# A four-image conv, state-space scan and expert layer on one core: the work beside the scans is cut finer and placed anew

## The chip, the cores and the metric

The kernel runs on one core of a Trainium2 chip. Five engines work side by side and meet at semaphores: PE (TensorE, matmuls and transposes into PSUM), DVE (VectorE), ACT (ScalarE), POOL (GpSimd) and SP, which here only issues DMAs. The metric is the device time of one execution in microseconds (us), as the median of several runs; a difference between two kernels is judged by such medians.

## The reference, cut to what matters

Input is `x` of 4 images of 32x32 pixels with 256 channels, all float32. Layer 0, the part that the change touches:

```python
x = layernorm(src) @ w_in + b_in              # 256 -> 512 channels
x = gelu(depthwise_conv_3x3(x, conv_w) + conv_b)
x = x.reshape(B, 1024, 512)
dt_raw, Bm, Cm = split(x @ w_x, [16, 80])     # 16 + 64 + 64 columns
dt = softplus(dt_raw @ w_dt + dt_bias)
def step(h, (xt, dtt, Bt, Ct)):               # over 1024 pixels, 64 states a channel
    h = exp(dtt * A) * h + (dtt * xt) * Bt
    return h, sum_n(h * Ct)
y = scan(step) + x * D_skip
out = src + layernorm(y) @ w_out + b_out
```

Layer 1 is an attention in matrix form and a mixture of 16 experts, two to a token. It follows layer 0, and the change leaves it alone.

## The kernel before

**Units and steps.** Each image is cut into two halves of 512 pixels, so there are 8 *units*, in order image by image. Units 0, 2, 4, 6 are first halves ("even"), units 1, 3, 5, 7 second halves ("odd"). Within a unit the 64 states are taken one after another: a *step* is one state n of one unit, 512 steps in all. Channels lie on the partitions in 4 groups of 128 (m = 0 to 3). A step therefore has 4 *slots*, one for each m, and a unit has 256 slots, numbered `at` in the code; `k` counts slots over all units.

**What one step does.** ACT makes `da = exp(dt*A)` for each m (`decay`, L901), 128x512. The input of the scan, `dt*x*B[n]`, is made row-major, in four row blocks j of 128 pixels, and then transposed by PE into a PSUM bank `ps` (`turn`, L908 and L913). A row block is scaled by ACT (`scale`, L881, tile `bx`, ten buffers). The first row block (j = 0) has three kinds: "A" it is scaled by ACT like the others; "P" it is scaled by POOL (`scale_apart`, L892, tile `bxp`); "D" it isn't scaled at all, but PE multiplies `dtxT` by a diagonal matrix of B that was written to DRAM and fetched again (`fetch_diagonal`, L873, tile `dgb`). DVE runs the scan itself, 128x512 (L927), from `da` and `ps` into `h`, a ring of four steps. After the fourth scan of a step POOL multiplies `h` by C (L934, 128x2048, with `cb_n`, which SP fetches as a broadcast of 256 KB a step). Eleven slots after a scan PE transposes `h` and sums it in four PSUM banks `y` (`add_up`, L948). There are three banks for `ps` and one, `bg`, for all work beside the scans, so that only one piece of that work can hold PSUM at a time.

**The work beside the scans.** While unit u is scanned, the inputs of later units are made: the layernorm and first product of a half image (`head`: ACT, PE, a copy, then PE and a copy into `pad`), the convolution as nine PE products a channel group with diagonal taps `dgc` (`conv`, L405) and its evacuation with bias (L417 or L419), gelu, then the projections for unit u+1 (`dt_bc`: product L456, copies `put_pair` L464, `put_low` L477, `put_bc` L488, then `dt_raw` L518, `put_dt` L528 and L529, exp, log, four sums of each m on POOL L560 to L566, and the turn to `dtxT` with copy L576). For unit u-1 it makes the layernorm's statistics (`after_stats`, L275) and the output product (`after`, L644 to L669). The last unit makes the attention's matrices instead.

**How it is put in order.** Nothing is left to a scheduler: the loop over k issues, slot by slot, `scale(k+8)`, `decay(k+4)`, `scan(k)`, `turn(k+3)`, `add_up(k-11)`, the fetches, and then as many *pieces* of the work beside as fit. Each piece has the smallest number of slots after its predecessor, an engine, a cost and a callable. `beside` lays each list of pieces evenly over a range of slots (`SKIP`, `HEAD1`, `CONV0`, `CONV1`, `HEAD0`, `STATS`, `DT`, `AFTER`); a piece goes out when its slot has come, its gap is over, what it needs is done, the `bg` bank is free if it takes it, and the costs already used on its engine in this slot leave room under `MOST`. Which engine makes a copy is read from `ODD` and `EVEN` through `on_scalar`:

```python
ODD, EVEN = ("pad", "xg", "yT", "dtx"), ("xg", "yT", "dtx")
CONV0, CONV1 = (50, 236), (22, 176)
DT = ((11, 38), (51, 64), (81, 93), (94, 184), (185, 240))
SUMS = (25, 51)
LAG = 11
FIRST, MOST = 11, 1.0
```

Kinds of the first row block follow a rule: in units up to 6, steps 25 to 50 are D and A in turn; elsewhere each fourth step is D and the rest P; D is A in unit 0. So units 1 to 6 have 13 A, 28 P and 23 D steps, unit 0 has 36 A and 28 P, unit 7 has 48 P and 16 D.

Of the kernel before, what the change touches and what calls it, by code (L numbers as in the profile page):

```python
# [16 lines left out]
P = 128  # L17
# [16 lines left out]
def conv_ssm_attn_moe_kernel(ctx: ExitStack, tc: tile.TileContext, a: dict, out: bass.AP):  # L34
# [106 lines left out]
    with ExitStack() as l0:  # L141
# [101 lines left out]
        EVERY = 2  # L243
        diag_b = [dram.tile([NS // EVERY, P, P], F32, name=f"diag_b{k}") for k in range(2)]
# [3 lines left out]
        def zero_diagonals(k):  # L248
            nc.sync.dma_start(
                out=diag_b[k].rearrange("n a b -> a n b"), in_=over_middle(zero, NS // EVERY)  # L250
            )
# [65 lines left out]
        def head(b, g, lo=0, hi=TPB):  # L317

            todo = [piece(1, "SP", 0, lambda: load_head(b, g))]

            def diagonal(i):
                t = pre.tile([P, P], F32, name="dg", tag="dg", bufs=2)
                i += g * TPB
                nc.scalar.activation(t, ident, AF.Copy, scale=rs_h[:, b, i : i + 1])
                i -= g * TPB
                made["dg", i] = t

            def turned(i, ck):
                if ck == 0:
                    take()  # L330
                nc.tensor.matmul(
                    made["bg"][:, blk(ck, P)], made["xt"][:, i, blk(ck, P)], made["dg", i],
                    start=True, stop=True,
                )

            def put(i):
                if i == lo:
                    made["xT"] = pre.tile([P, CK, BANK], F32, name="xT")
                nc.vector.tensor_copy(
                    made["xT"][:, :, blk(i, P)],  # L340
                    made["bg"][:, : CK * P].rearrange("p (k t) -> p k t", k=CK),
                )

            for i in range(lo, hi):
                todo.append(piece(6 if i == lo else 1, "ACT", 0.3, lambda i=i: diagonal(i)))
                for ck in range(CK):
                    todo.append(piece(
                        0 if ck else 2, "PE", 0.22, lambda i=i, ck=ck: turned(i, ck),
                        "" if ck else "take",
                    ))  # L350
                todo.append(piece(
                    2, "ACT" if on_scalar("xT") else "DVE", 0.42, lambda i=i: put(i), "free"
                ))

            def mult(m, ck):
                if ck == 0:
                    take()
                nc.tensor.matmul(
                    made["bg"][:, : (hi - lo) * P], w_in[:, ck, blk(m, P)],
                    made["xT"][:, ck, lo * P : hi * P], start=(ck == 0), stop=(ck == CK - 1),  # L360
                )

            def put_pad(m):
                pad = pads[m][:, 1 + g * ROWS + lo * RPT : 1 + g * ROWS + hi * RPT, 1 : 1 + WW]
                bg = made["bg"][:, : (hi - lo) * P].rearrange("p (h w) -> p h w", w=WW)
                if on_scalar("pad"):
                    nc.scalar.activation(pad, bg, AF.Identity, bias=b_in[:, m : m + 1])
                else:
                    nc.vector.tensor_scalar(pad, bg, b_in[:, m : m + 1], None, ALU.add)

            for m in range(DK):
                for ck in range(CK):
                    todo.append(piece(
                        1, "PE", 0.86, lambda m=m, ck=ck: mult(m, ck), "" if ck else "take"
                    ))
                todo.append(piece(
                    3, "ACT" if on_scalar("pad") else "DVE", 0.7, lambda m=m: put_pad(m), "free"
                ))
            return todo

        def conv(v):
# [19 lines left out]
            def tap(m, k):  # L401
                if k == 0:
                    take()
                i, j = divmod(k, 3)
                nc.tensor.matmul(  # L405
                    made["bg"].rearrange("p (h w) -> p h w", w=WW),
                    made["dgc", m * 3 + i][:, j, :],
                    pads[m][:, half * ROWS + i : (half + 1) * ROWS + i, j : j + WW],
                    start=(k == 0), stop=(k == 8),
                )  # L410
# [19 lines left out]
            for m in range(DK):  # L430
                for k in range(9):
                    if k % 3 == 0 and m * 3 + k // 3 + 2 < 3 * DK:
                        todo.append(piece(
                            0, "SP", 0, lambda q=m * 3 + k // 3 + 2: taps(q)
                        ))
                    todo.append(piece(
                        2, "PE", 0.86, lambda m=m, k=k: tap(m, k), "" if k else "take"
                    ))
                todo.append(piece(
                    3, "ACT" if on_scalar("xg") else "DVE", 0.69, lambda m=m: put(m), "free"  # L440
                ))
# [3 lines left out]
        def dt_bc(w, needs):  # L445
# [15 lines left out]
            def put_pair(j):  # L461
                if j == 0:
                    made["proj", w] = acts.tile([P, TPB, RX], F32, name="proj")
                nc.vector.tensor_copy(  # L464
                    made["proj", w][:, j : j + 2, :],
                    made["bg"][:, : 2 * RX].rearrange("p (j n) -> p j n", n=RX),
                )
# [8 lines left out]
            def put_low():  # L476
                nc.vector.tensor_copy(dtr[:R, :], made["bg"][:R, :])  # L477
# [8 lines left out]
            def put_bc():  # L486
                t = pre.tile([P, BANK], F32, name="bct")
                nc.vector.tensor_copy(t, made["bg"])  # L488
                cd = dram0.tile([NS, BANK], F32, name="cd")
                nc.sync.dma_start(out=cd, in_=t[NS:, :])  # L490
                if w > 0:
                    with nc.allow_non_contiguous_dma(reason="diagonals"):
                        nc.sync.dma_start(
                            out=diag_b[w % 2].rearrange("n a b -> n (a b)")[:, :: P + 1],
                            in_=t[:NS:EVERY, :P],
                        )
                made["cd", w] = cd

            for j in range(TPB):
# [5 lines left out]
                if j % 2:  # L505
                    todo.append(piece(3, "DVE", 0.5, lambda j=j: put_pair(j - 1), "free"))
            todo.append(piece(2, "PE", 0.44, turn_low, "take"))
            todo.append(piece(3, "DVE", 0.69, put_low, "free"))
            todo.append(piece(1, "PE", 0.44, turn_bc, "take"))
            todo.append(piece(3, "DVE", 0.69, put_bc, "free"))  # L510
# [5 lines left out]
            def dt_raw(m):  # L516
                take()
                nc.tensor.matmul(  # L518
                    made["bg"], w_dt[:, blk(m, P)], dtr, start=True, stop=True
                )  # L520
# [60 lines left out]
            for m in range(DK):  # L581
                todo.append(piece(1, "PE", 0.86, lambda m=m: dt_raw(m), "take"))
# [44 lines left out]
        def after(u, need):  # L627
# [44 lines left out]
            for j in range(TPB):  # L672
# [9 lines left out]
                for m in range(0, DK, 2):  # L682
                    todo.append(piece(
                        1, "PE", 0.88, lambda j=j, m=m: (mult(j, m), mult(j, m + 1)),
# [129 lines left out]
        def on_scalar(what):  # L814

            return not alone and what in (ODD if made["u"] % 2 else EVEN)
# [39 lines left out]
        def by_diagonal(s, j):  # L856

            u, n = steps[s]
            return j == 0 and u > 0 and n % (2 if summing(u, n) else 4) == 0

        def by_pool(s, j):

            u, n = steps[s]
            return j == 0 and n % 4 > 0 and not summing(u, n)

        def summing(u, n):

            return u + 1 < len(units) and SUMS[0] <= n < SUMS[1]

        def fetch_diagonal(s):  # L870
            u, n = steps[s]
            t = scanp.tile([P, P], F32, name="dgb", bufs=3)
            nc.sync.dma_start(out=t, in_=diag_b[u % 2][n // EVERY])  # L873
# [94 lines left out]
        def beside(u):  # L968
# [4 lines left out]
            made["u"] = u  # L973
            lists = [[([
                piece(1, "PE", 0.22, lambda m=m, j=j: skip(u, m, j))
                for m in range(DK) for j in range(TPB)
            ], SKIP)]]
            if v < n:
                b, half = units[v]
                if u == 0:  # L980
                    lists.append([
                        (head(b, 0), (11, 44)), (head(b, 1), (44, 77)), (conv(v), (77, 236)),
                    ])
                elif half == 0:
                    lists.append([(head(b, 1), HEAD1), (conv(v), CONV0)])
                else:
                    lists.append([(conv(v), CONV1)])
                    if b + 1 < NB:
                        lists[-1].append((head(b + 1, 0), HEAD0))
            if v == n:  # L990
                lists.append([(matrices(), MATS)])
            if u > 0:
                lists.append([(after_stats(u - 1), STATS)])
            if u + 1 < n:
                lists.append(list(zip(dt_bc(u + 1, ("st", u - 1) if u > 0 else None), DT)))
            else:
# [4 lines left out]
                ], DT[2])])  # L1001
            if u > 0:
                lists.append(list(zip(after(u - 1, ("rs", u - 1)), AFTER)))
# [7 lines left out]
        ODD, EVEN = ("pad", "xg", "yT", "dtx"), ("xg", "yT", "dtx")  # L1011

        SKIP = (11, 24)
        HEAD1, CONV0 = (14, 85), (50, 236)
        CONV1, HEAD0 = (22, 176), (200, 240)
        STATS = (11, 69)
        DT = ((11, 38), (51, 64), (81, 93), (94, 184), (185, 240))
        AFTER = ((36, 132), (139, 229))
        MATS = (44, 245)

        SUMS = (25, 51)
        SLOTS = NS * DK
        LAG = 11
        FIRST, MOST = 11, 1.0
        with tc.manual_schedule():
# [14 lines left out]
            for k in range(n_all + LAG):  # L1040
# [5 lines left out]
                if k < n_all:  # L1046
                    scan(*divmod(k, DK))
                    if k % DK == DK - 1 and k // DK + 4 < len(steps):
                        scale_apart(k // DK + 4)
                if k + 3 < n_all:  # L1050
                    turn(*divmod(k + 3, DK))
                if k >= LAG:
                    add_up(*divmod(k - LAG, DK))
# [16 lines left out]
                while True:  # L1070
                    best = None
                    for i, l in enumerate(lists):
# [7 lines left out]
                        if used[eng] > 0 and used[eng] + c > MOST:  # L1080
# [836 lines left out]
```

## Time and profile before

| | us |
|---|---|
| median of 3 runs | 3470.42 (3470.37 to 3471.43) |
| the profiled execution, its own time | 3483.06 |
| its span, first to last instruction | 3481.3 |
| before the first scan | 131.6 |
| scans, units 0 to 7 | 131.6 to 2718.3, that is 2586.7 |
| after the scans: layer 1 and output | 763.0 |

The profile lists for each engine what it executed and for how long. Busy time of an engine in a stretch of time is the union of its instructions; the mean of one is its own length, and two neighbours on ACT, DVE or PE can overlap a little, so that their starts lie closer than that length. Times in the trace count from the first instruction. The starts of the units' first scans are at 131.6, 459.0, 784.9, 1110.4, 1435.7, 1760.0, 2084.8 and 2408.0 us.

### The profile page before, as it was taken

Reading aid. Unit: us, or ns where it says so; the run is one execution under the profiler, and the core shown is the slowest. Engines: PE = TensorE matmul, PEld = TensorE weight load, DVE = VectorE, ACT = ScalarE, POOL = GpSimd, SP = SyncE. Lnnn points to the kernel's source line nnn. Section 1 sums busy time; section 2 is a strip of 40 time slices with the busy share of each in tenths; the row PEclk is TensorE's granted clock in tenths of the full one; section 3 lists DMA queues with packets and bytes.
Section 4 is the critical chain, followed back from the end, with each engine's and each line's share of the span. In section 5 each row is a group of like instructions: output and inputs, shape, how many; then the busy total and the mean of one; then the engine's idle time right before and its main releaser. Section 6 shows DMA issues by size and latency. Waiting matters only on the chain. (4 is left out here: it accounts for less than half of the span.)

```text
span 3481.3 us, 62766 instructions
## 1 busy us (share of the span) xinstructions
PE 3205.9 (92%) x23081; PEld 2718.2 (78%) x23081; DVE 2875.8 (83%) x3290; ACT 2680.8 (77%) x4525; POOL 2690.4 (77%) x1185
## 2 busy tenths in 40 slices
PE   7989999999999999999999999889999889699995
PEld 4677877888888888878888887778777666598994
DVE  4799999999999999999999999999999676422224
ACT  1799999998999899989999998999999454221211
POOL 0489988998999899989998999999999532133331
PEclk9999999999999999999999999999999999799997
DMA  3422222222332222223222223222212100699996
GB/s 102 110 61 67 65 64 70 70 72 63 77 74 63 69 76 72 63 64 79 74 68 68 69 65 75 60 62 66 61 62 69 56 19 19 235 325 307 322 308 227
DMA packets 413577, 347.81 MB, mean 100 GB/s; under 512 B 193345, under 2 KB 299841, under 8 KB 413266
## 3 DMA queue, kind: packets, MB, share of 16 engines
q1 hardware_dynamic: 393794, 319.97, 31.9%
q0 software_dynamic: 7104, 19.41, 1.7%
q10 hardware_dynamic: 12368, 4.37, 0.5%
q8 instruction: 185, 3.03, 0.4%
q14 instruction: 126, 1.03, 0.1%
HBM read 313.65 MB, written 29.47 MB: 99 GB/s over the span
## 5 line engine op out<-in xcount | busy, mean ns | idle before, releaser
L934 POOL TENSOR_TENSOR h<-h,cb_n 128x2048 f32<-128x2048 f32 x512 | 2145.2, 4198 | 139.3 <-DVE h L927 69.2
L901 ACT ACTIVATE da<-dt,l_conv_a_log_sb 128x512 f32<-128x512 f32 x2048 | 1434.6, 712 | 76.6 <-DVE h L927 74.4
L948 PE MATMUL y<-ident,h 128*128 128x128 f32 x8192 | 1236.3, 274 | 2.5 <-POOL h L934 2.5
L927 DVE TENSOR_TENSOR_SCAN h<-da,last,ps 128x512 f32<-128x512 f32 x1024 | 1218.5, 1266 | 19.5 <-PE ps L913 11.1
L927 DVE TENSOR_TENSOR_SCAN h<-da,ps 128x512 f32<-128x512 f32 x1024 | 1163.5, 1199 | 55.0 <-PE ps L913 26.5
L881 ACT ACTIVATE bx<-dtxT,proj 128x512 f32<-128x512 f32 x1650 | 1172.5, 711 | 22.4 <-DVE dtxT L576 16.4
L913 PE MATMUL ps<-ident,bx 128*128 128x128 f32 x6600 | 1073.1, 275 | 34.4 <-DVE h L927 18.8
L948 PEld LDWEIGHTS y<-ident,h 128*128 128x128 f32 x8192 | 967.4, 142 | 3.2 <-POOL h L934 3.2
L913 PEld LDWEIGHTS ps<-ident,bx 128*128 128x128 f32 x6600 | 791.1, 142 | 141.5 <-DVE h L927 58.5
L913 PE MATMUL ps<-ident,bxp 128*128 128x128 f32 x976 | 290.7, 298 | 78.6 <-DVE h L927 64.6
L1823 DVE TENSOR_TENSOR hT<-s,p 128x256 f32<-128x256 f32 x148 | 62.4, 422 | 340.9 <-ACT s L1822 340.9
L913 PEld LDWEIGHTS ps<-ident,bxp 128*128 128x128 f32 x976 | 137.0, 140 | 223.5 <-DVE h L927 107.4
L1817 PE MATMUL p<-xT,w 128*128 128x128 f32 x2368 | 292.2, 277 | 0.5 <-ACT xT L1806 0.5
L1817 PEld LDWEIGHTS p<-xT,w 128*128 128x128 f32 x2368 | 285.7, 194 | 4.9 <-ACT xT L1806 0.9
L1837 POOL DMA_INDIRECT yd<-yb,dst x74 | 73.0, 987 | 269.2 <-DMA yd<-yb,dst 172.3
L908 PE MATMUL ps<-dgb,dtxT 128*128 128x128 f32 x1232 | 261.2, 294 | 17.9 <-DVE h L927 12.0
L908 PEld LDWEIGHTS ps<-dgb,dtxT 128*128 128x128 f32 x1232 | 195.6, 191 | 94.7 <-DVE h L927 53.3
L1822 ACT ACTIVATE s<-p 128x256 f32<-128x256 f32 x148 | 56.9, 384 | 276.1 <-PE p L1817 276.1
L405 PE MATMUL bg<-pad,dgc 128*128 128x512 f32 x432 | 221.8, 595 | 3.5 <-DMA dgc<-diags 3.0
L892 POOL TENSOR_SCALAR bxp<-dtxT,proj 128x512 f32<-128x512 f32 x244 | 170.8, 700 | 59.2 <-DVE dtxT L576 59.2
L1829 PE MATMUL pf<-w,hT 128*128 128x256 f32 x592 | 153.3, 382 | 0.1
L1786 POOL DMA_INDIRECT xb<-xd,src x74 | 71.9, 972 | 97.8 <-DMA w<-in_L_ffn_w_dram 73.8
(308 smaller groups left out, 2351.0 us busy)
## 6 DMA issues: line engine op xcount, KB each, us to landing
cb_n<-cd SPq DMA_DIRECT2D x512, 256.0 KB, 3.2
w<-in_L_ffn_w_dram SPq DMA_DIRECT2D x222, 512.0 KB, 6.0
dgc<-diags SPq DMA_DIRECT2D x84, 192.0 KB, 3.2
dgb<-diag_b SPq DMA_DIRECT2D x154, 64.0 KB, 3.1
y<-yd SPq DMA_DIRECT2D x8, 1024.0 KB, 10.3
last<-h SPq DMA_DIRECT2D x256, 2.0 KB, 2.8
diag_b<-zero SPq DMA_DIRECT2D x2, 2048.0 KB, 9.3
xd<-xe SPq DMA_DIRECT2D x8, 512.0 KB, 2.9
```

Source lines behind the costliest of these rows:

```text
L405: nc.tensor.matmul(made["bg"].rearrange("p (h w) -> p h w", w=WW), made["dgc", m * 3 + i][:, j, :], pads[m][:, half * ROWS + i : (half + 1 ...
L881: nc.scalar.activation(t, made["dtxT", u][:, j, :], AF.Copy, scale=made["proj", u][:, j, R + n : R + n + 1])
L892: nc.gpsimd.tensor_scalar(t, made["dtxT", u][:, 0, :], made["proj", u][:, 0, R + n : R + n + 1], 1.0, ALU.mult, ALU.mult,)
L901: nc.scalar.activation(t, made["dt", u][:, m, :], AF.Exp, scale=A[:, m, n : n + 1])
L908: nc.tensor.matmul(t[:, blk(j, P)], made["dtxT", steps[s][0]][:, j, blk(m, P)], made["dgb", s], start=True, stop=True,)
L913: nc.tensor.transpose(t[:, blk(j, P)], made["bx", s, j][:, blk(m, P)], ident)
L927: nc.vector.tensor_tensor_scan(h[:, m, 1:], made.pop(("da", s, m)), made.pop(("dbx", s, m)), 0.0 if seg == 0 else last[b][:, n, m : m + 1] ...
L934: nc.gpsimd.tensor_tensor(h[:, :, :BANK], h[:, :, 1:], over_middle(made["c", s], DK), ALU.mult)
L948: nc.tensor.matmul(made["y", u][j][:, blk(m, P)], made["h", s][:, m, blk(j, P)], ident, is_transpose=True, start=n == 0 and m == 0, stop=n ...
L1817: nc.tensor.matmul(p12[:, j, s, :], on[w, i][:, ck, blk(h + j, P)], on["xT", i][:, ck, :], start=(ck == 0), stop=(ck == CK - 1),)
L1829: nc.tensor.matmul(on["pf", i], on["hT", i][:, hk, :], on["w3", i][:, hk, :], start=(hk == 0), stop=(hk == HK - 1),)
L1837: nc.gpsimd.indirect_dma_start(yd[:, :], bass.IndirectOffsetOnAxis(dst[:, i : i + 1], 0), yb, None)
```

## The change

It has seven parts.

1. **Finer PE pieces.** A tap of the convolution, a product of a whole head and a product of `dt_raw` are each cut in two pieces of 256 columns; a pair of products of `after` becomes two pieces of one. The two projections of a piece of `dt_bc` stay together. The part before the scans (`alone`) keeps whole pieces.
2. **Head rows.** ACT scales the 128x256 row block itself (`scaled_rows`) instead of making a 128x128 diagonal, and PE transposes the result instead of multiplying by the diagonal.
3. **Copies.** `APART` says for even and odd units which copies ACT makes. `bc`, `low` and `pair` move from DVE to ACT in both; `xg` moves from ACT to DVE in both; `dtx` moves from ACT to DVE in even units.
4. **Kinds.** `KINDS` lists the kind of each step's first row block, for even units, odd units and the last.
5. **Diagonals.** All 64 of a unit are kept in DRAM instead of each second one, so the two clearing transfers and each unit's diagonal write are twice as large.
6. **Slots.** `EVEN`, `ODD` and `START` (unit 0) give each list its own range of slots.
7. **Order and room.** `add_up(k-11)` is issued ahead of `turn(k+3)`. `MOST` differs by engine.

By these lists the counts of A, P and D steps are: unit 0 35, 29, 0; units 2, 4, 6 23, 29, 12; units 1, 3, 5 26, 21, 17; unit 7 30, 21, 13.

```diff
-        EVERY = 2
-        diag_b = [dram.tile([NS // EVERY, P, P], F32, name=f"diag_b{k}") for k in range(2)]
+        diag_b = [dram.tile([NS, P, P], F32, name=f"diag_b{k}") for k in range(2)]
...
-            def diagonal(i):
-                t = pre.tile([P, P], F32, name="dg", tag="dg", bufs=2)
...
-                nc.scalar.activation(t, ident, AF.Copy, scale=rs_h[:, b, i : i + 1])
...
+            def scaled_rows(i):
+                t = pre.tile([P, C], F32, name="xn", tag="dg", bufs=2)
+                r = g * TPB + i
+                nc.scalar.activation(
+                    t, made["xt"][:, i, :], AF.Copy, scale=rs_h[:, b, r : r + 1]
+                )
+                made["xn", i] = t
...
+                nc.tensor.transpose(made["bg"][:, blk(ck, P)], made["xn", i][:, blk(ck, P)], ident)
...
+            cut = [(lo, hi)] if alone else [(lo, (lo + hi) // 2), ((lo + hi) // 2, hi)]
...
-                    made["bg"].rearrange("p (h w) -> p h w", w=WW),
+                    made["bg"].rearrange("p (h w) -> p h w", w=WW)[:, blk(c, deep), :],
                     made["dgc", m * 3 + i][:, j, :],
-                    pads[m][:, half * ROWS + i : (half + 1) * ROWS + i, j : j + WW],
-                    start=(k == 0), stop=(k == 8),
+                    pads[m][:, at : at + deep, j : j + WW],
+                    start=(k == 0 and c == 0), stop=(k == 8), skip_group_check=True,
...
-                    todo.append(piece(
-                        2, "PE", 0.86, lambda m=m, k=k: tap(m, k), "" if k else "take"
-                    ))
+                    for c in range(parts):
+                        todo.append(piece(
+                            1, "PE", 1.03 / parts, lambda m=m, k=k, c=c: tap(m, k, c),
+                            "" if k or c else "take",
+                        ))
...
-                            in_=t[:NS:EVERY, :P],
+                            in_=t[:NS, :P],
...
-            return j == 0 and u > 0 and n % (2 if summing(u, n) else 4) == 0
+            return j == 0 and u > 0 and KINDS[kind_of(u)][n] == "D"
...
+        APART = (
+            ('bc', 'low', 'pair', 'yT'),
+            ('bc', 'dtx', 'low', 'pad', 'pair', 'yT'),
+        )
+        KINDS = (
+            'DPPPDPPPAPPPAPPPAAPAAPPPPAPAPAPAADADDAAADAAAADADDAAADPPPDPPPDPPP',
+            'DPPPAAPAAAPAPPPAPPPAAAPAADADDADAADADADADADADADADDADPAPPPDPPPDPAP',
+            'ADADAAPAAAPAAAPAAAPADAPADAAAAPPPDAPADAPADAPAADADDPPPDPPPDPPPDAPA',
+        )
+        EVEN = {
+            'skip': (18, 66),
+            'head': (23, 91),
+            'conv': (47, 210),
+            'stats': (11, 61),
+            'dt0': (15, 21),
+            'dt1': (50, 60),
+            'dt2': (93, 97),
+            'dt3': (31, 103),
+            'dt4': (102, 214),
+            'after0': (45, 89),
+            'after1': (144, 207),
+        }
+        ODD = {
+            'skip': (13, 18),
+            'head': (179, 234),
+            'conv': (14, 172),
+            'stats': (23, 50),
+            'dt0': (17, 22),
+            'dt1': (61, 77),
+            'dt2': (90, 108),
+            'dt3': (45, 157),
+            'dt4': (221, 226),
+            'after0': (11, 104),
+            'after1': (114, 222),
+        }
...
+            'conv': (43, 228),
...
+            'dt3': (122, 188),
...
-        FIRST, MOST = 11, 1.0
+        FIRST = 11
+        MOST = {'PE': 2.1, 'DVE': 0.8, 'ACT': 1.1, 'POOL': 1.0, 'SP': 9.0}
...
+                if k >= LAG:
+                    add_up(*divmod(k - LAG, DK))
                 if k + 3 < n_all:
                     turn(*divmod(k + 3, DK))
-                if k >= LAG:
-                    add_up(*divmod(k - LAG, DK))
```

## The prediction

> **What bounds the kernel now.** I read the page's busy shares first: PE 92, DVE 83, ACT 77, POOL 77 per cent. No engine is full, yet four are nearly so, and the second part shows why: nines on all four from slice 3 to 31, which are the scans. The change touches only these, apart from eight head rows ahead of them. So I asked for busy time by unit and then by quarters of a unit (64 slots each).
>
> By unit (busy us of PE, weight loads, DVE, ACT, POOL), units 6 and 7:
>
> ```profile
> core 0: us, PE busy (x) PEld busy (x) DVE busy (x) ACT busy (x) POOL busy (x), PEclk, DMA share, GB/s
> ...
> 2084.80:2408.00 323.20, 293.65 (x2307) 259.93 (x2308) 319.43 (x297) 300.88 (x486) 304.21 (x117) 0.97 0.28 65
> 2408.00:2718.30 310.30, 290.28 (x2219) 243.43 (x2217) 308.22 (x272) 280.81 (x450) 308.58 (x123) 1.00 0.21 62
> ```
>
> DVE idles 3.8 and 2.1 us there: both are bound by DVE. In the same answer DVE's idle is 21.4, 18.3 and 18.2 us in units 0, 2, 4, and 7 us in units 1, 3, 5. The sum is 2586.7 - 2501.1 = 85.6 us. That idle is all that a better order can win. Quarters of unit 1, then of unit 2:
>
> ```profile
> 459.00:542.60 83.60, 78.76 (x625) 69.45 (x623) 82.04 (x80) 75.35 (x122) 75.77 (x30) 1.00 0.27 70
> 542.60:627.50 84.90, 81.35 (x582) 66.47 (x581) 82.30 (x74) 79.35 (x126) 77.44 (x32) 1.00 0.24 71
> 627.50:707.00 79.50, 76.78 (x588) 66.23 (x587) 76.93 (x67) 79.41 (x126) 79.50 (x30) 1.00 0.23 67
> 707.00:784.90 77.90, 75.71 (x601) 67.56 (x600) 77.58 (x71) 77.11 (x129) 77.08 (x30) 1.00 0.23 72
> ```
>
> ```profile
> 784.90:870.30 85.40, 78.17 (x624) 70.03 (x623) 82.56 (x88) 75.02 (x121) 75.16 (x29) 0.98 0.30 65
> 870.30:953.90 83.60, 81.80 (x591) 67.93 (x590) 78.56 (x75) 78.57 (x126) 78.20 (x32) 1.00 0.30 73
> 953.90:1031.30 77.40, 77.33 (x599) 68.31 (x598) 72.91 (x67) 76.48 (x125) 75.98 (x28) 1.00 0.30 74
> 1031.30:1110.40 79.10, 75.26 (x585) 67.32 (x584) 73.17 (x67) 75.68 (x120) 78.80 (x30) 0.98 0.29 70
> ```
>
> The reader is to see that the bound moves. In the first quarter DVE is full and ACT and POOL have 8 to 10 us to spare. In the second half of unit 2 DVE idles 4.5 and 5.9 us while PE, ACT or POOL is full. Whom DVE waits for, over the scans:
>
> ```profile
> DVE h L927 <- PE ps L913: 37.7, 130, 1.2
> DVE h L927 <- ACT da L901: 20.4, 28, 3.7
> DVE h L927 <- ACT bx L881: 10.2, 18, 2.9
> ```
>
> PE's part is many short waits (130, none over 1.2 us), ACT's few long ones. In the timeline such a PE wait looks like this:
>
> ```profile
> 1006.66 1.02 PE L405 MATMUL bg<-pad,dgc 128*128 128x512 f32 x2
> ...
> 1007.52 0.60 PE L913 MATMUL ps<-ident,bx 128*128 128x128 f32 x4
> ...
> 1008.33 5.69 DVE L927 TENSOR_TENSOR_SCAN h<-da,ps 128x512 f32<-128x512 f32 x5 [0.49 <-PE ps L913]
> ```
>
> A tap of the convolution holds PE for 0.86 us, the transposes for the next scan come behind it, and DVE stands for 0.49. I went through all waits of the timeline: 32 of the 37.7 us follow a tap begun within 3.5 us. Taps at their mean spacing would cover about half of the time, so the link is more than chance.
>
> [...] two 256-column products (L658) from 933.99 to the next start at 934.86 are 0.43 each, half of a 512-column tap (940.31 to 941.17, 0.86). [...]
>
> **The change part by part.**
>
> *Kinds.* An A step instead of D or P costs one more scaling on ACT. Its record is 0.711 us, but beside its neighbours it takes 0.61 (an exp starts at 1011.38, the scaling after it at 1011.99). Odd units have 13 more A: +8.0 us of ACT; 7 fewer P of 0.70: -4.9 of POOL. Units 2 and 4 have 10 more A: +6.2 of ACT; POOL +0.7; 11 fewer D, a little less PE. Unit 7: 30 more A, 27 fewer P, on an engine pair that DVE outlasts: nothing.
>
> *Copies.* Each unit that makes projections loses from DVE two `pair` (0.43 each), `low` 0.65, `bc` 0.66: -2.17. Convolution units gain four `xg` (0.69, nearest row L369 at 0.72): +2.76. Even units gain four `dtx` (0.66): +2.64. Net DVE: +0.6 in odd units 1, 3, 5, +3.2 in units 0, 2, 4, +0.5 in 6: about +12 us that must fit into idle. ACT loses 0.65 for each `xg`, 0.57 for each `dtx`, and gains about 2.0 for the copies (two of 0.57[...]).
>
> *Slots, with the above, by quarter* (counted from the order in which both programs issue). Unit 2: the first quarter goes from 22 pieces on DVE to 14: the four copies (2.17) and half of `put_dt` (four of 0.69) leave, -4.9, and DVE is the bound there. The second quarter takes 2.75 of that; it has 5.0 DVE idle, but ACT gets four more scalings: +0.5. The third takes three `xg` and three `dtx`, 4.1 us into 4.5 idle: +0.8. The fourth has less on ACT: -1.2. Sum -4.8, for units 2 and 4 -9.6. Odd unit: first quarter -1.5 (copies out, one `xg` in), second +1.0 (five more scalings and `bc` on ACT, +3 into 5.5 idle), third +0.5 (two more POOL sums of 1.28 where POOL is full, but it enters less late, as 5.4 us leave its second quarter), fourth -0.5. Sum -0.5, three times -1.5. Unit 0: -3.4 by the same count (ACT -2.3 in the fourth quarter, -1 in the third, -1.2 in the second, +1.1 in the first from its copies and longer rows). Unit 6 +0.5. Together -14.0.
>
> *Pieces.* A half tap holds PE for 0.43, so a late transpose is late by half. PE's work is the same. Of the 32 us with taps, between nothing (the backlog, not the piece, makes PE late) and 25 could go; I take -9, about what halving leaves after the part that the quarters have already counted. The heads' transposes save PE about 0.9 a head and cost ACT 4 x 0.1: nothing.
>
> *Order.* `add_up` ahead of `turn` only rotates the loop: pieces now stand between `turn` and the next `add_up`. It takes one slot, 1.2 us, from POOL's slack. PE waited 0.3 us for POOL in all of the scans, so the cover is there: 0, with +3 a unit if POOL's denser sums use it up.
>
> *Diagonals.* Both rows are in the page or the DMA view:
>
> ```profile
> diag_b<-zero SPq DMA_DIRECT2D x2, 2048.0 KB, 9.3
> diag_b<-bct SPq DMA_DIRECT2D x7, 16.0 KB, 7.4
> ```
>
> From 140 to 160 us the DMA engines are 90 to 102% busy with the clearings, and SP stands 6.3 us on the issue of `last` at 150.59, behind the second. Twice the bytes at the 250 GB/s seen end near 170 us, where step 7's multiply wants its `cb_n`: 0 to +10, I take +2. A diagonal write fills the DMA engines from 190 to 195; twice that delays a `cb_n` fetched three steps (14.6 us) ahead that lands in 3.2: 0, at most +3 each.
>
> Sum: -14.0 - 9 + 2 = -21. The profiled execution took 3483.1, 12.7 above the median; against it 3462, against the median **3449**.
>
> **The rivals.** *B, the idle nearly goes.* If order and pieces bring units 0 to 5 to the 3 us of units 6 and 7, idle falls from 85.6 to about 25, and 12 of added DVE work stays: -48, 3422. For it: DVE's excess sits where others are idle. Against it: POOL and ACT stay at 95 per cent. *C, given back.* If half taps bring nothing and the clearings and POOL's denser third quarter (unit 0 puts all 16 sums into 66 slots) take 10: -4, 3466. *D, slower: ACT becomes the bound in odd units.* ACT is busy 311.2 of unit 1; +8.0 scalings - 2.6 + 2.0 + 0.4 is 319.0. Of its 14.7 idle only 6.8 is full buffers (`da` waiting for DVE); 7.9 is waiting for products, 3.6 of it the exp of L535 on DVE. That makes 326.9 in a unit of 325.9. From the point where these 7.9 us don't shrink, each microsecond of ACT is the unit's: +7.8 three times, the gain of units 2 and 4 lost to the same late `da`, and the rest as above without the taps: +23 + 2 - 3 = +22; 3 a unit taken off for the lead that ACT can win in the first quarter, where it idles 8 us, leaves +13, 3483. That lead (six `da` buffers) is also what speaks against it.
>
> **How the numbers follow.** The forecast 0.54, B 0.14, C 0.13, D 0.19. A measurement here tells about 0.2% (7 us) from no change: faster 0.68, same 0.13, slower 0.19. The forecast's own range is 3436 to 3462. To hold 8 in 10 it reaches to B below and to D's centre above: 3424 to 3482.
>
> **What would show it.** Right: units 2 and 4 near 320, first quarters near 80; odd units within 1 us of before; DVE's wait for PE near 25; DVE idle about 53. Wrong: ACT idle in odd units near zero with DVE waiting for `da`; PE waiting for POOL at L948's successor; POOL idle at step 7 of unit 0; or waits for PE unchanged with half taps.

## The result and the profile after

The changed kernel takes 3438.97 us (median of 4 runs, 3435.89 to 3446.1) against 3470.93 us of the kernel before on the same chip: a ratio of 0.9907 with a 95% interval of 0.9887 to 0.9926, that is 32 us less. The profiled execution is the slowest of the four, 3446.1 us.

Busy shares first, after:

```profile
PE 3180.6 (92%) x23385; PEld 2757.0 (80%) x23385; DVE 2882.1 (84%) x3302; ACT 2714.7 (79%) x4611; POOL 2662.0 (77%) x1141
```

They hardly differ from before, as the work is nearly the same. Then busy time by unit, after, units 0 to 2, 6 and 7:

```profile
core 0: us, PE busy (x) PEld busy (x) DVE busy (x) ACT busy (x) POOL busy (x), PEclk, DMA share, GB/s
130.50:458.50 328.00, 303.32 (x2334) 270.39 (x2334) 310.70 (x290) 315.91 (x503) 299.37 (x106) 0.98 0.39 88
458.50:779.60 321.10, 310.81 (x2455) 280.40 (x2453) 318.38 (x287) 314.48 (x509) 304.32 (x111) 1.00 0.28 70
779.60:1097.80 318.20, 306.57 (x2434) 277.99 (x2433) 310.31 (x295) 310.65 (x501) 308.78 (x119) 1.00 0.34 70
...
2056.60:2378.40 321.80, 293.81 (x2273) 253.02 (x2270) 314.87 (x298) 307.37 (x500) 308.08 (x119) 0.98 0.32 64
2378.40:2684.40 306.00, 287.80 (x2189) 239.04 (x2188) 305.86 (x271) 291.71 (x474) 288.46 (x95) 1.00 0.20 61
```

DVE idles 2.7 us in unit 1 and 7.9 in unit 2, but 17.3 in unit 0. By unit, from the start of one unit's first scan to the next (the list of starts given with the profile before is up to 3 us early from unit 4 on; this table has the starts as the trace has them):

| us | 0 | 1 | 2 | 3 | 4 | 5 | 6 | 7 | sum |
|---|---|---|---|---|---|---|---|---|---|
| before | 327.4 | 325.9 | 325.5 | 326.5 | 325.3 | 324.9 | 324.3 | 307.0 | 2586.8 |
| after | 328.0 | 321.1 | 318.2 | 321.6 | 317.5 | 319.7 | 321.8 | 306.0 | 2553.9 |

The gain lies in units 1 to 5: 7 to 8 us in the even, 5 in the odd. Unit 0 gained nothing. A quarter of a unit (64 slots) that two kernels have in common takes nearly the same time in both traces (the second one of units 1, 3 and 5, for example, is 84.6 us each time in this kernel and in two of those below), so a microsecond in a unit can be read from single traces. The third quarter of unit 6 is the exception: the granted clock falls to half there (to 0.50, for about 14 us from 2231 in the changed kernel and for about 10 from 2290 in the kernel before), and in two kernels below that quarter takes 93.6 and 95.9 us instead of 85 to 89. DVE's busy time over the scans rose from 2501.1 to 2506.6 us, its idle fell from 85.6 to 2553.9 - 2506.6 = 47.3. Whom DVE waits for during the scans, after (engine, line and operation that waits, releaser, us in total, times, longest):

```profile
DVE h L950 <- ACT da L924: 10.3, 19, 2.3
DVE h L950 <- PE ps L936: 9.8, 39, 2.0
DVE h L950 <- DMA last<-h: 7.4, 4, 2.9
DVE h L950 <- PE y L971: 3.7, 1, 3.7
DVE h L950 <- ACT bx L904: 3.6, 12, 0.6
```

PE's 37.7 became 9.8, ACT's 30.6 became 13.9, and the 6.0 us of `ysb` waiting for `y` (L965 for L948 in the trace of before) are gone. Two rows are new. `last<-h` is the 2 KB store of a step's last column, which a first half leaves to the second. `h` holds four steps, so a scan can take the place of the step four back only when that step's column has been stored. The one wait of 3.7 us put down to PE `y` is of the same kind: it is the first scan of step 7 in unit 0, which started at 171.52; the sum of step 3, whose place it takes, had ended at 168.52, but the store of step 3 landed at 171.40. In the kernel with the old order below, the trace puts this scan's wait down to the store:

```profile
DVE h L950 <- DMA last<-h: 5.2, 1, 5.2
```

### The profile page after: what moved, and what is told of

It reads as the page before. It is cut to its first block, busy times and chain, and to the rows that moved or that the text cites. A ratio compares the mean times of both kernels' runs of the same rounds, so it can differ in the third digit from the quotient of the medians.

```text
span 3444.3 us, 63146 instructions
## 1 busy us (share of the span) xinstructions
PE 3180.6 (92%) x23385; PEld 2757.0 (80%) x23385; DVE 2882.1 (84%) x3302; ACT 2714.7 (79%) x4611; POOL 2662.0 (77%) x1141
## 5 line engine op out<-in xcount | busy, mean ns | idle before, releaser
L904 ACT ACTIVATE bx<-dtxT,proj 128x512 f32<-128x512 f32 x1748 | 1244.0, 712 | 29.6 <-DVE dtxT L596 17.0
L950 DVE TENSOR_TENSOR_SCAN h<-da,ps 128x512 f32<-128x512 f32 x1024 | 1170.3, 1203 | 37.7 <-ACT da L924 9.7
L936 PE MATMUL ps<-ident,bx 128*128 128x128 f32 x6992 | 1118.0, 275 | 41.8 <-DVE h L950 28.7
L971 PEld LDWEIGHTS y<-ident,h 128*128 128x128 f32 x8192 | 980.4, 141 | 99.4 <-issue 20.3
L936 PEld LDWEIGHTS ps<-ident,bx 128*128 128x128 f32 x6992 | 819.1, 142 | 101.6 <-DVE h L950 80.1
L936 PE MATMUL ps<-ident,bxp 128*128 128x128 f32 x800 | 237.6, 297 | 53.6 <-DVE h L950 41.0
L409 PE MATMUL bg<-pad,dgc 128*128 128x256 f32 x864 | 258.2, 380 | 0.5 <-DMA dgc<-diags 0.5
L936 PEld LDWEIGHTS ps<-ident,bxp 128*128 128x128 f32 x800 | 112.0, 140 | 139.1 <-DVE h L950 84.2
L931 PE MATMUL ps<-dgb,dtxT 128*128 128x128 f32 x800 | 171.0, 296 | 22.0 <-DMA dgb<-diag_b 9.7
L915 POOL TENSOR_SCALAR bxp<-dtxT,proj 128x512 f32<-128x512 f32 x200 | 140.6, 703 | 60.5 <-DVE dtxT L596 60.5
L931 PEld LDWEIGHTS ps<-dgb,dtxT 128*128 128x128 f32 x800 | 120.8, 191 | 48.9 <-DVE h L950 35.2
## 6 DMA issues: line engine op xcount, KB each, us to landing
diag_b<-zero SPq DMA_DIRECT2D x2, 4096.0 KB, 16.8
y<-yd SPq DMA_DIRECT2D x8, 1024.0 KB, 10.1
```

The source lines that it names most:

```text
L409: nc.tensor.matmul(made["bg"].rearrange("p (h w) -> p h w", w=WW)[:, blk(c, deep), :], made["dgc", m * 3 + i][:, j, :], pads[m][:, at : at ...
L904: nc.scalar.activation(t, made["dtxT", u][:, j, :], AF.Copy, scale=made["proj", u][:, j, R + n : R + n + 1])
L915: nc.gpsimd.tensor_scalar(t, made["dtxT", u][:, 0, :], made["proj", u][:, 0, R + n : R + n + 1], 1.0, ALU.mult, ALU.mult,)
L931: nc.tensor.matmul(t[:, blk(j, P)], made["dtxT", steps[s][0]][:, j, blk(m, P)], made["dgb", s], start=True, stop=True,)
L936: nc.tensor.transpose(t[:, blk(j, P)], made["bx", s, j][:, blk(m, P)], ident)
L950: nc.vector.tensor_tensor_scan(h[:, m, 1:], made.pop(("da", s, m)), made.pop(("dbx", s, m)), 0.0 if seg == 0 else last[b][:, n, m : m + 1] ...
```

## Experiments

Each is one kernel. Ratios are to the kernel before, run on the same chip; brackets hold 95% intervals.

**Pieces whole again, everywhere.** The changed kernel with its PE pieces uncut, a whole tap one slot after the other:

```diff
-            cut = [(lo, hi)] if alone else [(lo, (lo + hi) // 2), ((lo + hi) // 2, hi)]
+            cut = [(lo, hi)]
-            parts = 1 if alone else 2
+            parts = 1
-            raw = 1 if alone else 2
+            raw = 1
```

(`after` also issues its products in pairs again.)

> The changed kernel with whole PE pieces (part 1 undone: 512-column taps, head and dt_raw products, pairs in the output product), slots, kinds, copies and order as changed. Theory T (finer pieces and balance share the gain, as forecast): +9 to +15 us on the changed kernel's 3439, about 3450, and DVE's waits for PE `ps` over the scans back from 9.9 to 20-25 us. Rival R1 (the finer pieces are all of it): back to about 3470, waits for `ps` near 38. Rival R2 (balance is all of it): within 3 us of 3439, waits near 10.

Measured: 1.0086 [1.0072, 1.01], 3503.56 us, slower than before. DVE's waits for PE, in this kernel:

```profile
DVE h L950 <- PE ps L936: 67.6, 124, 4.1
```

All three forecasts missed, but this tells nothing of the piece size. With the gap of 1 left in place, taps of 0.86 us came in each slot instead of each second, twice the rate of the kernel before. What it shows is that PE's work per slot has a price.

**Half taps alone.** The kernel before with each tap cut in two, one slot apart, so that a tap still takes two slots:

```diff
-                    todo.append(piece(
-                        2, "PE", 0.86, lambda m=m, k=k: tap(m, k), "" if k else "take"
-                    ))
+                    for c in range(parts):
+                        todo.append(piece(
+                            1, "PE", 0.86 / parts, lambda m=m, k=k, c=c: tap(m, k, c),
+                            "" if k or c else "take",
+                        ))
```

> The kernel before with only the taps of the convolution cut in two (each half one slot after the last, in place of two slots for a whole one). T: -9 to -12, about 3460, waits of DVE for PE `ps` from 38 to about 27. R1: -25 to -32, about 3440. R2: no change, 3468 to 3473.

Measured: 1.0025 [1.0016, 1.0034], 3482.3 us. The visible waits fell as the forecast had it, yet the kernel became 9 us slower:

```profile
DVE h L933 <- PE ps L919: 21.5, 71, 4.1
```

DVE's busy time over the scans rose from 2501.1 to 2516.5 us with the same work. The timeline of this kernel in unit 2 shows where that went (start, us, line, instructions run together, idle before them in brackets):

```profile
897.73 5.66 DVE L933 TENSOR_TENSOR_SCAN h<-da,ps 128x512 f32<-128x512 f32 x5
...
914.88 2.54 DVE L933 TENSOR_TENSOR_SCAN h<-da,ps 128x512 f32<-128x512 f32 x2 [0.29 <-PE ps L919]
917.62 1.22 DVE L933 TENSOR_TENSOR_SCAN h<-da,ps 128x512 f32<-128x512 f32 x1 [0.20 <-ACT bx L887]
...
951.43 5.05 DVE L933 TENSOR_TENSOR_SCAN h<-da,ps 128x512 f32<-128x512 f32 x4 [0.18 <-ACT da L907]
```

A scan's record is 1.22 us. Five on time take 5.66, so they start (5.66 - 1.22) / 4 = 1.11 apart and overlap by 0.11. The four at 951.43 start (5.05 - 1.22) / 3 = 1.28 apart, each 0.17 late, and the view lists no idle between them: a scan that is late by less than 0.11 only loses its overlap, and the shortest gap listed here is about 0.17. Over units 0, 2 and 4 the mean spacing of scans between which no idle is listed went from 1.124 us in the kernel before to 1.150. And the stretch shows why cutting cannot help there. PE's busy time in 46.18 us, the kernel before and then this one:

```profile
core 0: us, PE busy (x), PEclk, DMA share, GB/s
914.76:960.94 46.18, 46.18 (x335) 1.00 0.34 86
```

```profile
914.76:960.94 46.18, 46.18 (x364) 1.00 0.34 84
```

PE has no gap in either. The ends of matmuls are modelled in the profile, but the starts say the same. With half taps:

```profile
919.64 0.60 PE L919 MATMUL ps<-ident,bx 128*128 128x128 f32 x4
920.08 0.60 PE L954 MATMUL y<-ident,h 128*128 128x128 f32 x4
920.52 0.60 PE L409 MATMUL bg<-pad,dgc 128*128 128x256 f32 x2
920.95 0.60 PE L919 MATMUL ps<-ident,bx 128*128 128x128 f32 x4
```

Transposes, sum and half tap take 0.44 us each, 1.31 a slot, and none of them waits for anything. With a whole tap each second slot, PE takes 2.61 for two slots (from the tap at 918.52 in the kernel before to the next at 921.13): the same pace, slower than the 1.11 at which scans can follow each other. In the kernel before, 125 of the 130 waits for PE (34 of 37.7 us) end a stretch of 6 us in which PE idled less than 2 per cent; of all stretches of that length in the scans 58 per cent are like that. Where PE is full, its work for a slot sets the pace, and halves only spread the lateness over more scans. That explains why nothing was won, not the 9 us that were lost. A little of them is PE's own: from the start of a tap to the next start there are 0.864 us on average for a whole one and 0.877 for two halves, an estimated 3 us over the 216 taps of the scans. The rest is open.

**Whole taps, two slots apart.** The changed kernel with this alone undone:

```diff
-            parts = 1 if alone else 2
+            parts = 1
...
-                            1, "PE", 1.03 / parts, lambda m=m, k=k, c=c: tap(m, k, c),
+                            2, "PE", 1.03 / parts, lambda m=m, k=k, c=c: tap(m, k, c),
```

> The changed kernel with whole taps two slots apart, as the kernel before had them; all other pieces stay fine. The first run with whole pieces put its whole taps one slot apart, so PE had 0.87 + 0.86 us in slots of 1.2. T (half taps are worth 9 to 15): 3448 to 3454, waits for `ps` 20 to 25. Rival R6 (what cost 65 us there was the rate of the taps, not their size): within 4 us of 3439.

Measured: 0.9908 [0.9892, 0.9924], 3440.09 us: the changed kernel's own ratio. Its visible waits for PE are 2.4 times those of the changed kernel,

```profile
DVE h L950 <- PE ps L936: 23.4, 80, 0.5
```

but its scans start 1.129 us apart in units 0, 2 and 4, where those of the changed kernel start 1.142 apart (the last run's forecast has 1.138 and 1.147 for the two, by another count). Both ways the waits were the wrong measure. The units show something that the medians can't tell: units 1 to 5 together are 5.3 us shorter with half taps than with whole ones, while half taps in the kernel before made the same units 6.5 us longer. So what halves are worth depends on the slots and the order around them.

**The order alone, taken back and put in.** First the changed kernel with `turn` ahead of `add_up` as before:

```diff
-                if k >= LAG:
-                    add_up(*divmod(k - LAG, DK))
                 if k + 3 < n_all:
                     turn(*divmod(k + 3, DK))
+                if k >= LAG:
+                    add_up(*divmod(k - LAG, DK))
```

> The changed kernel with `turn` ahead of `add_up` again (half of part 7 undone). T (a rotation, no cost either way): within 3 us of 3439. Rival R5 (after its pieces PE is late, and then it matters that the transposes for the next scan come first or last): 6 us or more to either side, seen in DVE's waits for `ps`.

Measured: 0.9939 [0.9925, 0.9953], 3454.25 us, 0.0032 or 11 us slower than the changed kernel (the intervals just touch). And the kernel before with `add_up` moved ahead, nothing else:

> The kernel before with `add_up` ahead of `turn`, nothing else. T: -6 to -11, ratio 0.997 to 0.998, the waits of `ysb` gone. R8: no change, or slower, since pieces then stand between `turn` and `add_up` at old slots.

Measured: 0.9967 [0.9958, 0.9977], 3462.24 us, 11.5 us faster than before by this ratio. Taken back, it brings back a row in the waits,

```profile
DVE ysb L988 <- PE y L971: 6.2, 7, 1.0
```

which the kernel before has as well (6.0, 7 times) and the two kernels with the new order don't. Its place in the timeline, just after the last scan of unit 0, in the kernel before:

```profile
470.73 1.25 DVE L927 TENSOR_TENSOR_SCAN h<-da,last,ps 128x512 f32<-128x512 f32 x1
...
472.04 0.33 PE L913 MATMUL ps<-ident,bxp 128*128 128x128 f32 x1
472.21 0.49 PE L913 MATMUL ps<-ident,bx 128*128 128x128 f32 x3
472.53 0.60 PE L948 MATMUL y<-ident,h 128*128 128x128 f32 x4
...
472.84 1.29 DVE L965 COPY ysb<-y 128x512 f32<-128x512 f32 x2 [0.86 <-PE y L948]
```

and in the changed kernel:

```profile
470.90 0.60 PE L971 MATMUL y<-ident,h 128*128 128x128 f32 x4
...
471.37 1.27 DVE L988 COPY ysb<-y 128x512 f32<-128x512 f32 x2
471.51 0.14 PEld L936 LDWEIGHTS ps<-ident,bxp 128*128 128x128 f32 x1 [0.25 <-DVE h L950]
```

In both stretches PE runs its matmuls in the order of issue. Before, the last sum of a unit stood behind the transposes of a `turn` that waited for a scan to free its bank, and DVE, next in whose queue was the copy of that sum, stood 0.86 us. Now the sum goes first and the copy has no wait. Seven unit ends make 6.0 us. The other 5 or so are spread over the scans (units 1 to 5 of the changed kernel are 0.5 to 2.6 us shorter with the new order, 0.9 of it this copy). What PE itself waits for points to a reason. Transposes that wait for a scan to free their bank held it for 83.4 us before and for 65.6 with the order alone, in which PE has done the sum by then:

```profile
PE ps L913 <- DVE h L927: 83.4, 131, 9.5
```

```profile
PE ps L913 <- DVE h L927: 65.6, 129, 9.5
```

That the other 5 us come from there isn't shown.

**Slots alone, then slots and copies, then the order too.** The kernel before with `EVEN`, `ODD` and `START` of the change and the old copies:

```diff
+        APART = (("xg", "yT", "dtx"), ("pad", "xg", "yT", "dtx"))
```

> The kernel before with the new slots alone (part 6), whole pieces, old copies, kinds, order and room. T (balance between the quarters is worth 14 us by the forecast, some of it through the copies): -8 to -14, 3460; DVE idle falls in the first quarters' neighbours. Rival R1 (slots help only with finer pieces): 3470 or above, with DVE's waits for PE `ps` above 40 us.

Measured: 0.9992 [0.9979, 1.0004], 3473.2 us: no change that can be told. With the change's `APART` as well (and the three copies of `dt_bc` choosing their engine by it):

```diff
-        APART = (("xg", "yT", "dtx"), ("pad", "xg", "yT", "dtx"))
+        APART = (('bc', 'low', 'pair', 'yT'), ('bc', 'dtx', 'low', 'pad', 'pair', 'yT'))
```

> As the last, with the new copies too (parts 3 and 6). T: -12 to -18, 3456, first quarters of even units near 80. Rival R4 (the copies only add 12 us to a full DVE): slower than the last by 5 to 12.

Measured: 0.9964 [0.9951, 0.9977], 3462.03 us, 12.5 us faster by this ratio. In the traces unit 0 is 8.5 us shorter for it, unit 6 6.3, units 2 and 4 2.3 and 2.1; units 1, 3, 5 and 7 change by -0.6 to +1.7. With the order too:

> The kernel before with the new slots, copies and `add_up` ahead of `turn` (parts 3, 6 and half of 7). T (the order gives its 11 us here too, 6 of them the waits of `ysb` for the last `add_up` at seven unit ends): 0.9964 falls to 0.993, 3450, and DVE's 6.0 us for PE `y` are gone. Rival R7 (the order is all that parts 1, 2 and 7 give): down to the 0.989 of the run with old kinds. Rival R8 (the order helps only with the fine pieces): stays at 0.996.

Measured: 0.9907 [0.989, 0.9923], 3440.88 us. So parts 3 and 6 with the first half of part 7 give as much as the whole change; the product of the ratios of slots with copies and of the order is 0.9931, a little less. Slots pay only with the copies; copies alone weren't run, so whether they need the slots isn't known.

**Old kinds and half the diagonals.** The changed kernel with the old rule for the first row block, so that `diag_b`, its clearing and its writes are half as large:

```diff
-        diag_b = [dram.tile([NS, P, P], F32, name=f"diag_b{k}") for k in range(2)]
+        diag_b = [dram.tile([NS // 2, P, P], F32, name=f"diag_b{k}") for k in range(2)]
...
-            return j == 0 and u > 0 and KINDS[kind_of(u)][n] == "D"
+            return j == 0 and u > 0 and n % (2 if summing(u, n) else 4) == 0
```

> The changed kernel with the old rule for the kinds of the first row block and with every second diagonal (parts 4 and 5 undone). T: the kinds are part of the balance, and giving them up costs 12 to 20 us, of which the halved diagonals give 10 back: 3441 to 3449. Rival (kinds do nothing, only their diagonals cost): about 3425 to 3430. Rival R3 (kinds carry most of the gain): above 3455.

Measured: 0.989 [0.9874, 0.9907], 3431.13 us, 7.8 us less than the changed kernel (the intervals overlap), and by unit 317.9, 323.3, 318.7, 323.3, 318.7, 321.8, 316.4, 306.0. The new kinds are worth about 2 us in each odd unit and 1 in units 2 and 4, together 7.7, and the change pays 10.1 in unit 0 and 5.4 in unit 6.

**Clearings earlier.** The changed kernel with both clearings issued ahead of the scans, beside the work that comes before them:

```diff
+            zero_diagonals(1)
+            zero_diagonals(0)
...
-                if k in (4, 14):
-                    zero_diagonals(1 if k == 4 else 0)
```

> The changed kernel with both clearings of the diagonals issued right after the first four fetches of C, before the scans, instead of at slots 4 and 14. T (the doubled clearings cost unit 0 about 9 us of DVE idle in slots 16 to 32, where the head's rows wait behind them): unit 0 from 328 to about 319, in all 3430. Rival (ACT and POOL limit unit 0 anyway): unit 0 stays within 2 us, 3437 to 3440.

Measured: 0.9909 [0.9894, 0.9924], 3442.44 us, as the changed kernel. Unit 0 went from 328.0 to 317.4 us, but the first scan from 130.5 to 148.6. SP's issues of the taps' diagonals from 80 to 140 us (shortest, median and longest in ns), in this kernel:

```profile
L398 SPq DMA_DIRECT2D dgc<-diags x9: 319/473/10169, 92.6 to 133.7; - x9
```

One stands 10.2 us behind the clearings, and the convolution with it. So the clearings cost unit 0 about 10 us, and this place costs as much: 18.1 us before the first scan against 15.4 won in the scans. All of the 10 lie in the first quarter of unit 0, 85.5 us in the changed kernel and 74.9 here; the other three quarters agree within 0.1. Where they stand in the changed kernel, the timeline of unit 0 reads:

```profile
153.54 0.60 SPq L248 DMA_DIRECT2D diag_b<-zero  x1
154.23 14.70 SPq L962 DMA_DIRECT2D last<-h  x1
...
158.76 0.51 ACT L323 ACTIVATE xn<-xt,rs_h 128x256 f32<-128x256 f32 x1 [6.15 <-DMA xt<-in_x_dram]
```

The 2 KB store of `last` behind the second clearing holds SP for 14.7 us, and the fetch of `xt`, issued at 152.37 between the two clearings, makes ACT wait 6.15. Before, the same store stood 6.3. Unit 0's 10 us can be followed to DVE's waits. The first scan of step 5 stood 2.0 us and started at 154.81; the store of step 1, behind the first clearing, had landed at 154.69 (the trace puts this wait down to PE). Then come 2.3 us behind ACT, 3.7 for the store above (step 7), and at 210.89 another 2.1, for a store behind the unit's diagonal write, which was issued at 195.44 and landed at 210.59.

**Clearings in eight parts, diagonal writes in four, the old kinds in unit 6.** The rest is the changed kernel:

```diff
-                if k in (4, 14):
-                    zero_diagonals(1 if k == 4 else 0)
+                if k % DK == 3 and (k < 32 or 64 <= k < 96):
+                    zero_diagonals(1 if k < 32 else 0, k % 32 // DK)
...
+            if w > 0:
+                for i in range(4):
+                    todo.append(piece(4, "SP", 0, lambda i=i: put_diagonals(i)))
```

> The changed kernel with the clearings in eight parts each, one part a step (the second clearing 64 slots later), each unit's diagonal write in four parts four slots apart, and the old kinds in unit 6. T (the doubled diagonals cost about 10 us in unit 0 and 2 to 5 in later units, through transfers queued behind them): 3421 to 3427, unit 0 near 318, no wait of DVE for `last`. Rival: nothing but unit 0 changes, 3430.

Measured: 0.985 [0.9832, 0.9869], 3420.81 us: 18 us less than the changed kernel, 53 less than the kernel before beside it (3474.2). Units 0, 1, 2 and 6 of this kernel:

```profile
core 0: us, PE busy (x) PEld busy (x) DVE busy (x) ACT busy (x) POOL busy (x), PEclk, DMA share, GB/s
128.20:444.90 316.70, 298.20 (x2334) 268.17 (x2334) 310.22 (x290) 315.03 (x503) 299.37 (x106) 0.99 0.38 91
444.90:766.00 321.10, 310.67 (x2455) 280.44 (x2453) 318.43 (x288) 314.54 (x509) 304.34 (x111) 1.00 0.25 70
766.00:1082.20 316.20, 305.86 (x2433) 277.99 (x2432) 310.00 (x295) 310.28 (x501) 309.02 (x119) 1.00 0.31 70
...
2039.90:2356.90 317.00, 294.67 (x2317) 259.09 (x2314) 314.98 (x297) 302.22 (x489) 307.55 (x118) 0.98 0.29 67
```

and its waits over the scans:

```profile
DVE h L956 <- PE ps L942: 7.5, 37, 0.3
DVE h L956 <- ACT da L930: 6.0, 18, 1.3
DVE h L956 <- ACT bx L910: 3.0, 12, 0.4
```

Unit 0 is 11.3 us shorter with DVE, ACT and POOL busy as long as in the changed kernel, unit 6 4.8, unit 2 2.0, and no row of `last` is left. The bytes are the same: what changed is the length of one transfer and where it stands. In unit 6 kinds and the split write changed together; of its 4.8 us, 2.9 was one wait for `last` in the changed kernel. The kinds show in the third quarter of the unit: of the kernels built on the changed one, and leaving out the two long quarters named above, those with the new kinds take 88.3 to 88.9 us there, those with the old ones 84.7 to 85.8.

**The same with whole taps, two slots apart.**

> As the last, with whole taps two slots apart. From the earlier pair (0.9907 with half taps, 0.9908 with whole ones) the same time within 4 us, with more visible DVE idle for `ps` and shorter scans back to back (1.138 against 1.147 us in units 0, 2, 4).

Measured: 0.9874 [0.985, 0.9898], 3424.44 us. Half taps are ahead here by 3.6 us between the medians and by 8 between the ratios, and the intervals overlap. In the traces units 1 to 5 are 5.2 us shorter with them, as in the pair above (5.3).

## Why the prediction was right, and which of its terms were not

The forecast, 3449 us and faster, was right in sign and 10 us too high. Its stage was right too: the gain is DVE idle, units 2 and 4 came out at 318.2 and 317.5 (near 320 forecast), their first quarters at 79.6 and 78.7 (near 80), and DVE idle at 47.3 (53 forecast). The terms of the sum were not.

- *Balance, -14.0.* Slots with copies gave -12.5, the right size, but not in the right place: -9.6 was counted for units 2 and 4 and -3.4 for unit 0, and the trace has -4.4 and -8.5, with another -6.3 in unit 6, where +0.5 was counted. So the size is luck in part. Odd units were forecast at -0.5 and gained 5: about 2 from the kinds and 2 from the order. Of the 2.0 us that ACT was to gain for the copies, the share of the two `pair` was the author's estimate, as the kernel before makes them on DVE (0.43 us, L464). In the changed kernel a `pair` takes ACT 0.39 us (L470), `low` and `bc` 0.56 each (L483, L496), 1.9 together. The other prices stand in the trace of before: a copy of 512 columns out of `bg` takes 0.65 to 0.67 us on DVE (L477, L488) and 0.56 to 0.59 on ACT (L576, L650).
- *Pieces, -9.* By the medians nothing that can be told (0.9908 with whole taps against 0.9907), by the traces of both pairs about -5, and half taps alone made the kernel before slower. The sum priced visible waits; its lower bound, that the backlog and not the piece makes PE late, describes the kernel before. That tap and wait stand side by side was true of 32 us (the 3.5 us behind each tap cover about 24 per cent of the scans, not the half that was taken), and no proof: PE was full there with either size.
- *Order, 0.* **This is the step that failed most.** It was argued as a rotation of the loop whose only price was POOL's slack. A rotation changes which instruction stands ahead of which in PE's queue, and a row of 6.0 us, `ysb` waiting for `y`, stood in DVE's waits just below those shown. Measured: -11 to -12. Nor was DVE's idle time all that an order could win: with the order alone it fell by 9.0 us in the scans and DVE's busy time by 5.9. POOL's slack mostly held: PE's waits for its products at the sums rose from 0.3 to 3.1 us.
- *Diagonals, +2 (0 to +10).* The upper end: about +10 in unit 0, by three kernels whose unit 0 takes 316.7 to 317.9 (one has the old kinds there too). The reason given was that POOL's step 7 would want its `cb_n`; step 7 was among those that waited, but what was held was SP's queue and, through it, `xt` and `last`. Slots, copies and order win about 10 us in unit 0 (317.8 us with the old clearings, against 327.4), and the doubled clearings took them back. The 2 KB store issued at 154.23 behind the 4 MB landed at 171.40. The diagonal writes, taken as 0, cost a little as well: of the 7.4 us of waits for `last`, 5.4 lie in units 2, 4 and 6, and the kernel with split writes has none.
- *Heads, `dt_raw`, pairs of `after`, head rows and `MOST`.* Costed at nothing; slots, copies and order without them and without half taps equal the changed kernel, which also bears some 8 us of kinds and diagonals. Together they may give back about that much, the half taps about 5 of it by the traces; the intervals don't allow saying so.

The sum therefore came out near by chance: -9 for the pieces, of which at most about 5 can be seen, stands for -11 that was costed at 0. Of the rivals, D (ACT becomes the bound in odd units) fell: ACT is busy 314.5 of 321.1 us in unit 1, close, but DVE idles only 2.7. C had both its premises about right, pieces that bring little and clearings that take 10, and missed by 27 us, as it too put the order at 0. B, idle down to about 25 and a time of 3422, is what the kernel with split clearings reached (idle 2534.8 - 2505.7 = 29).

Open: what the 5 us of the order beyond the unit ends are, why half taps gain about 1 us a unit in one setting and lose as much in the other, and why order, slots and copies together give slightly more than their product.

## What to carry to other kernels

Before a wait is priced as a gain, ask whether the engine waited for was full: here 125 of 130 waits were of that kind, and smaller pieces alone made the kernel slower (1.0025). When two blocks of a loop swap places, read each queue's order at the turn of a unit, where a short sum can stand behind a long wait (here DVE stood 0.86 us for one), and look for its row in the waits. A long transfer off the critical path may be worth cutting when small ones follow it in the same queue, even if its bytes stay: here that gave about 11 us (unit 0 from 328.0 to 316.7).

## What the runs showed of the hardware that was not expected

- Scans of 128x512 with records of 1.20 to 1.22 us follow each other at 1.11 when their inputs are there, so lateness up to about 0.11 us counts as busy time. In odd units, where a scan starts from a column of `last`, records are about 1.27 us and the spacing is 1.17.
- A clearing of 4 MB lands in 16.8 us (2 MB: 9.3), and the issue of a 2 KB store soon after it holds SP 14.7 us (6.3 before). In eight parts of 512 KB, one a step, it cost unit 0 nothing that could be seen: 316.7 us, against 317.8 with slots, copies, order and the old clearings.
